# A gated cross-attention and mixture-of-experts block: first batch in halves, last batch's shared gate and up as seven products

## The chip, the cores and the metric

The kernel runs on one core of one Trainium2 chip. The metric is device time in microseconds (us). A core has TensorE (PE; its weight loads are listed apart as PEld), VectorE (DVE), ScalarE (ACT), GpSimd (POOL) and SyncE (SP, which here issues most DMAs). Each engine works through its own instructions in order and waits for the others through semaphores.

## The reference

All data are float32. Four batches of 512 tokens of width 512 go through two sub-blocks, each behind a layer norm and with a residual:

```python
x = x + jnp.tanh(g_xattn[0]) * _L0_xattn_ref(_layernorm(x), fside, ctx)
x = x + jnp.tanh(g_ffn[0]) * _L0_ffn_ref(_layernorm(x), gate_w, w_gate, w_up, w_down, ws_gate, ws_up, ws_down)
```

The first is, for each batch with weights of its own, two linears that are quantised to int8 steps (with a smoothing scale from column maxima and row scales), with silu(gate) * up between them. The second is a mixture of 16 experts over all 2048 tokens together, two experts a token, at most 256 tokens an expert, plus a shared expert that every token passes:

```python
g = jax.nn.silu(jnp.einsum('ech,ehi->eci', buf, w_gate))
u = jnp.einsum('ech,ehi->eci', buf, w_up)
expert_out = jnp.einsum('eci,eih->ech', g * u, w_down)
...
sh = jnp.einsum('ti,ih->th', jax.nn.silu(x @ ws_gate) * (x @ ws_up), ws_down)
```

The shared expert has 704 hidden features: five full chunks of 128 and a rest of 64.

## The kernel before

**Stages.** (1) The opening, batch 0's two linears and its second norm, written out by hand as steps with due times (`opening.at(time, ...)`, sorted and emitted). (2) The middle, batches 1 to 3, whose order a planner fixes while the program is built: each step has an engine, a duration, its needs and a rank, and `Plan` starts from the times at which each engine is taken to come free (`dict(PE=74.5, DVE=76.5, ACT=74.0, POOL=78.0, ...)`). The chain of a batch (first linear, second linear, norm, routing) has low ranks, so it goes first; the shared expert's products of batches 0 to 2 have the highest and fill TensorE between. (3) Sixteen routed experts. (4) The last stage: the shared expert of batch 3, the gathering of the routed results by GpSimd, their addition to X, and the stores.

**Opening, end of the second linear.** For each of four tiles of 128 tokens: `multiplied` (L726, TensorE), `scale` (L732, DVE), `residual` (L739, X + o, on GpSimd unless given DVE), `stats` (L292 and L293, DVE). Then `inv_std` (L270) gives 1/std for all four tiles at once: `begin` on DVE, a square root on ScalarE (L266), `end` on DVE. `normal` (L753, DVE) writes y, `turn_y` transposes it on TensorE (L773) and copies it on ScalarE into xT (L354). Between them `idle` (L1266) emits transposes that nobody reads. Only when all four tiles are in xT does `beside` run the first chunk of the shared expert, four products for gate (pg) and four for up (pu, both L972), each over 512 token columns, with silu (L976) and hT = g * pu (L979). Steps of batch 1's first linear stand among these products: column maxima of x and of its weights (`turn_max`, `wide1.turn`, L299), the smoothing scales s and rs (L316 to L325), their row broadcasts (`row_rs`, `row_s`, L307), then `divide` (L494, DVE) and `multiply` (L499, GpSimd).

**Between middle and experts.** When the last batch is routed, `tokens_of` (L930) sums one-hot products on TensorE into st; DVE turns that into slot_token (L944), GpSimd gathers the tokens of expert 0 (L1105), a DMA transposes them (L391), ScalarE and DVE join them into xgT (L354), and DVE forms sums S of them (L1144 to L1147). A routed expert's gate and up are seven half-size products each over 352 columns (L1154, `gate_up`), with sums on DVE and copies on ScalarE between them: a 2 by 2 block product by seven multiplications.

**Last stage.** Chunk 0 of batch 3's shared expert runs whole. Then 20 buffers are filled by gathers (L1699), the gates of chunks 1 to 4 and the rest (L1011) run, then the four ups, each followed by additions of gathered results (`add_results(upto)`, L1710, counted through 12, 15, 18, 21) and by its hT. The token products (sh, L1037, and L1043 for the rest) follow in two pairs of tiles, with additions up to 28 and 32 and `tokens_add` (L1050) with the stores (L1682). A gather beyond the twentieth is issued when an addition frees a buffer:

```python
def add_results(upto):
    while added[0] < upto:
        j, k = tiles[added[0] // 2], added[0] % 2
        vec.scalar_tensor_tensor(X[:, j, :], yks[added[0]], wk[k][:, j : j + 1], X[:, j, :], ALU.mult, ALU.add)
        if k == 1 and j < NT - TT:
            store(j)
        added[0] += 1
        if len(yks) < 2 * NT:
            gather_result()
```

Of the kernel before, what the change touches and what calls it, by code (L numbers as in the profile page):

```python
# [20 lines left out]
P = 128  # L21
# [99 lines left out]
def flamingo_gated_kernel(  # L121
# [138 lines left out]
    def small(n, name):  # L260
        return stat.tile([P, n], F32, tag=name, name=name)
# [8 lines left out]
    def inv_std(w, h, table=False):  # L270


        def begin():
            w.ve, w.r = small(TT, "ve" + h), small(TT, "r" + h)
            vec.tensor_scalar(w.ve, w.mv[:, :, 1], LN_EPS, None, ALU.add)

        def end():
            if table:
                vec.reciprocal(w.r, w.r)

            c = small(TT, "c" + h)
            vec.tensor_tensor(c, w.r, w.r, ALU.mult)
            vec.scalar_tensor_tensor(c, c, -0.5, w.ve, ALU.mult, ALU.mult)
            vec.scalar_tensor_tensor(w.r, c, 1.5, w.r, ALU.add, ALU.mult)
            w.nmr = small(TT, "nmr" + h)
            vec.scalar_tensor_tensor(w.nmr, w.mv[:, :, 0], -1.0, w.r, ALU.mult, ALU.mult)

        return [begin, lambda: root(w.r, w.ve, neg_half, table), end]
# [151 lines left out]
    def first(b):  # L440
# [27 lines left out]
        def turn_max():  # L468
            v.tp = columns(beside_ps if b == 1 else ps, v.am, HC)
# [146 lines left out]
    def second(b):  # L616
# [190 lines left out]
        v.norm = inv_std(v, "2", table=b == 0)  # L807
        return v
# [154 lines left out]
    def glu_steps(xT, o, dst, home):  # L963


        pl, bufs = home
        v = SimpleNamespace(ps={})

        def product(name, w, k):
            if k == 0:  # L970
                v.ps[name] = ps_mm.tile([P, H], F32, tag="mm", name=name)
            pe.matmul(v.ps[name], lhsT=w[:, k, o : o + P], rhs=xT[:, k, :], start=(k == 0), stop=(k == HC - 1))  # L972

        def silu():
            v.g = pl.tile([P, S], F32, tag="g", name="g", bufs=bufs)
            act.activation(v.g, v.ps["pg"], AF.Silu)  # L976

        def times():
            vec.tensor_tensor(dst, v.g, v.ps["pu"], ALU.mult)  # L979

        gate = [lambda k=k: product("pg", wsg, k) for k in range(HC)]
        up = [lambda k=k: product("pu", wsu, k) for k in range(HC)]
        return gate, silu, up, times
# [7 lines left out]
    def shared(b, done=None):  # L991
        s = SimpleNamespace()

        def chunk_steps(c, home=(shp, 2)):
            if c == 0:
                s.hT = shp.tile([P, len(CHUNKS_IS), S], F32, tag="hT", name="hT")
            return glu_steps(xTs[b], c * P, s.hT[:, c, :], home)
# [254 lines left out]
    f1, (wide1, narrow1) = first(1), weights(1, beside_ps)  # L1252
# [4 lines left out]
    def each(step, *args, ts=range(TT)):  # L1257
        return [lambda t=t: step(t, *args) for t in ts]
# [9 lines left out]
    def idle_x(t):  # L1268
        idle(X[:, t, :])
# [31 lines left out]
    opening.at(53.5, lambda: s0.product(2), lambda: s0.residual(1), lambda: s0.stats(0), lambda: s0.product(3))  # L1301
    opening.at(55.0, lambda: s0.residual(3, vec), lambda: s0.residual(2), lambda: s0.stats(1), lambda: s0.stats(3))
    opening.at(55.1, *each(idle_x, ts=[1, 2, 3]))
    opening.at(58.0, lambda: s0.stats(2), s0.norm[0], *each(lambda t: idle(s0.mv[:, t, 0:1]), ts=[1, 3]), lambda: idle(s0.mv[:, 2, 0:1], 3), s0.norm[1], s0.norm[2], lambda: idle(s0.ve[:, :1], 3))
    for t in range(TT):
        opening.at(61.0 + 0.5 * t, lambda t=t: s0.normal(t, vec), lambda t=t: s0.turn_y(t))
    sh0 = shared(0)

    opening.at(64.0, *each(f1.greater, ts=[1, 2, 3]), *each(wide1.absolute), *each(wide1.greater, ts=[1, 2, 3]))

    def beside():
        gate, silu, up, times = sh0.chunk_steps(0)
        order = gate[:1] + [f1.turn_max] + gate[1:3] + [f1.column_max] + gate[3:] + [wide1.turn, wide1.end]
        order += f1.smooth + [lambda: table(AF.Silu), silu]
        order += up[:2] + [f1.row_rs, f1.row_s, *each(f1.multiply), *each(f1.divide)] + up[2:] + [times]
        for step in order:
            step()


    opening.at(65.0, beside, lambda: s0.keep_normal(TT - 1), lambda: s0.store_normal(TT - 1))  # L1320
    with tc.manual_schedule():
# [5 lines left out]
        dict(PE=74.5, DVE=76.5, ACT=74.0, POOL=78.0, SP=70.0, DMA=70.0, XBAR=70.0),  # L1327
# [257 lines left out]
    plan_shared(0, sh0, [], range(1, FULL), home0)  # L1585
# [101 lines left out]
    with tc.manual_schedule():  # L1687
        chunks = [sh3.chunk_steps(0)]
        for step in chunks[0][0] + [chunks[0][1]] + chunks[0][2] + [chunks[0][3]]:
            step()  # L1690
# [31 lines left out]
        for c in range(1, FULL):  # L1722
            chunks.append(sh3.chunk_steps(c, (results, 4)))
            for step in chunks[c][0] + [chunks[c][1]]:
                step()
# [3 lines left out]
        for c, upto in zip(range(1, FULL), (12, 15, 18, 21)):  # L1729
            for step in chunks[c][2]:  # L1730
                step()
            add_results(upto)
            chunks[c][3]()
            if c == 2:
                sh3.rest_times(0)
                sh3.rest_times(1)

        for u, uptos in enumerate(((28, 28), (2 * NT, 2 * NT))):
# [49 lines left out]
```

## Time and profile before

| what | us |
|---|---|
| runs shown, lowest / median / highest | 576.94 / 586.7 / 592.93 |
| the profiled execution | 580.96 |
| its span | 579.0 |
| busy in the span: PE / DVE / ACT / POOL | 538.2 / 406.4 / 228.0 / 140.8 |
| batch 0's first shared product begins | 63.22 |
| last stage, first product to last addition | 512.13 to 576.12 |

Busy time of TensorE counts each product from its start to a modelled end, so products that follow each other overlap in it: the distance from start to start tells what one costs. A product in float32 appears as two passes, two records. Granted clock is the share of TensorE's full clock. "a <- b" in a list of waits means that a waited for b: us in total, times, longest. A releaser named "issue" or "remote" is one that the profile couldn't name.

### The profile page before, as it was taken

Reading aid. Unit: us, or ns where it says so; the run is one execution under the profiler, and the core shown is the slowest. Engines: PE = TensorE matmul, PEld = TensorE weight load, DVE = VectorE, ACT = ScalarE, POOL = GpSimd, SP = SyncE. Lnnn points to the kernel's source line nnn. Section 1 sums busy time; section 2 is a strip of 40 time slices with the busy share of each in tenths; the row PEclk is TensorE's granted clock in tenths of the full one; section 3 lists DMA queues with packets and bytes.
Section 4 is the critical chain, followed back from the end, with each engine's and each line's share of the span. In section 5 each row is a group of like instructions: output and inputs, shape, how many; then the busy total and the mean of one; then the engine's idle time right before and its main releaser. Section 6 shows DMA issues by size and latency. Waiting matters only on the chain.

```text
span 579.0 us, 5971 instructions
## 1 busy us (share of the span) xinstructions
PE 538.2 (93%) x1830; PEld 283.9 (49%) x1830; DVE 406.4 (70%) x927; ACT 228.0 (39%) x379; POOL 140.8 (24%) x155
## 2 busy tenths in 40 slices
PE   0667799999999999999989999999999999999977
PEld 0544444544444444544455555555555555644422
DVE  6889788999998997985478666665755665315445
ACT  4554577538516353140146254444443444211000
POOL 1315032253261511201321022111111100027740
PEclk9978999999999999999999999999999999999989
DMA  8971012013205092010787999999999995336864
GB/s 283 366 243 37 1 73 72 1 44 82 57 1 109 15 326 68 2 72 3 169 253 219 219 284 282 250 269 271 291 241 261 287 259 144 86 101 199 247 216 164
DMA packets 93967, 95.07 MB, mean 164 GB/s; under 512 B 51552, under 2 KB 70240, under 8 KB 93936
## 3 DMA queue, kind: packets, MB, share of 16 engines
q1 hardware_dynamic: 84064, 69.39, 45.1%
q0 software_dynamic: 5120, 16.78, 9.2%
q10 hardware_dynamic: 4752, 8.52, 3.9%
q8 instruction: 15, 0.25, 0.2%
q14 instruction: 16, 0.13, 0.1%
HBM read 66.36 MB, written 16.78 MB: 144 GB/s over the span
## 4 chain that ended last, share of the span: by engine, by line
PE 75%; DVE 12%; issue 5%; POOL 3%; ACT 1%; DMA 1%; another core or an unknown queue 1%; SPq 0%; DVEq 0%; POOLq 0%
PE b L1154 22%; PE eo L987 14%; PE pg L972 9%; PE sh L1037 9%; PE pu L972 8%; POOL yk L1699 2%; PE pr L1011 2%; PE tp_h L1174 2%; PE acc L576 2%; DVE X L1710 1%; PE rowb L307 1%; PE sh L1043 1%; DVE scx L331 1%; PE acc L726 1%
## 5 line engine op out<-in xcount | busy, mean ns | idle before, releaser
L987 PE MATMUL eo<-wd,ehT 128*128 128x512 f32 (+1 forms) x192 | 85.1, 592 | 0.0
L1105 POOL DMA_INDIRECT xg<-xn_dram,slot_token x32 | 35.7, 1117 | 195.4 <-DMA xp<-xg 160.6
L1037 PE MATMUL sh<-wsd,hT 128*128 128x512 f32 x160 | 75.3, 607 | 4.0 <-DVE hT L979 4.0
L972 PE MATMUL pg<-xT,wsg 128*128 128x512 f32 x160 | 74.9, 597 | 0.7 <-ACT xT L354 0.7
L972 PE MATMUL pu<-xT,wsu 128*128 128x512 f32 x160 | 74.0, 595 | 0.0
L987 PEld LDWEIGHTS eo<-wd,ehT 128*128 128x128 f32 (+1 forms) x192 | 36.4, 190 | 41.6 <-issue 37.0
L354 ACT COPY xgT<-xp 128x1024 int16<-128x1024 int16 x31 | 39.5, 1339 | 27.6 <-DMA xp<-xg 27.6
L1203 DVE TENSOR_TENSOR p<-p,b 128x352 f32<-128x352 f32 x16 | 8.3, 520 | 57.6 <-PE b L1154 57.6
L1037 PEld LDWEIGHTS sh<-wsd,hT 128*128 128x128 f32 x160 | 29.5, 194 | 36.2 <-issue 30.5
L1699 POOL DMA_INDIRECT yk<-eo_dram,slot x32 | 32.6, 1020 | 51.5 <-PE pg L972 42.1
L972 PEld LDWEIGHTS pu<-xT,wsu 128*128 128x128 f32 x160 | 29.2, 190 | 30.8 <-issue 30.6
L972 PEld LDWEIGHTS pg<-xT,wsg 128*128 128x128 f32 x160 | 28.7, 190 | 31.0 <-issue 29.5
L1154 PE MATMUL b<-T,S 128*128 128x352 f32 x128 | 40.6, 460 | 0.7 <-DVE S L1145 0.7
L1154 PE MATMUL b<-wg,xgT 128*128 128x352 f32 x128 | 40.6, 460 | 0.0
L1154 PE MATMUL b<-wu,S 128*128 128x352 f32 x128 | 40.5, 459 | 0.0
L1165 ACT COPY eo_sb<-eo 128x512 f32<-128x512 f32 x32 | 18.7, 585 | 47.4 <-PE eo L987 39.4
L979 DVE TENSOR_TENSOR hT<-g,pu 128x512 f32<-128x512 f32 x20 | 13.6, 682 | 32.1 <-PE pu L972 15.6
L1154 PEld LDWEIGHTS b<-T,S 128*128 128x128 f32 x128 | 24.2, 190 | 14.5 <-issue 1.2
L1154 PEld LDWEIGHTS b<-wu,S 128*128 128x128 f32 x128 | 24.3, 190 | 13.5
L499 POOL TENSOR_TENSOR wi<-wi,s_row 128x512 f32<-128x512 f32 x16 | 19.9, 1272 | 42.5 <-ACT s_row L484 42.5
L1154 PEld LDWEIGHTS b<-wg,xgT 128*128 128x128 f32 x128 | 23.1, 190 | 10.9 <-issue 0.8
L1710 DVE SCALAR_TENSOR_TENSOR X<-yk,wk,X 128x512 f32<-128x512 f32 x32 | 23.4, 751 | 7.0 <-DMA yk<-eo_dram,slot 6.5
(235 smaller groups left out, 866.0 us busy)
## 6 DMA issues: line engine op xcount, KB each, us to landing
wg<-in_L_ffn_w_gate_dram SPq DMA_DIRECT2D x16, 704.0 KB, 7.7
wu<-in_L_ffn_w_up_dram SPq DMA_DIRECT2D x16, 704.0 KB, 6.3
wd<-in_L_ffn_w_down_dram SPq DMA_DIRECT2D x16, 512.0 KB
eo_dram<-eo_sb ACTq DMA_DIRECT2D x32, 256.0 KB, 2.0
X<-in_x_dram SPq DMA_DIRECT2D x16, 256.0 KB, 6.5
xn_dram<-yp SPq DMA_DIRECT2D x16, 256.0 KB, 2.0
out_dram<-X SPq DMA_DIRECT2D x15, 256.0 KB, 2.0
wi<-in_fside_BxS2xS_dram SPq DMA_DIRECT2D x3, 1024.0 KB
```

What stands on the lines that cost most here:

```text
L354: return (vec.tensor_copy if on is vec else act.copy)(dst, src)
L499: on.tensor_tensor(w.wi[:, t, :], w.wi[:, t, :], v.s_row, ALU.mult)
L576: pe.matmul(accs[t], lhsT=block(b, w.xqT, k, t), rhs=block(b, w.wqT, k), start=(k == 0), stop=(k == HC - 1))
L972: pe.matmul(v.ps[name], lhsT=w[:, k, o : o + P], rhs=xT[:, k, :], start=(k == 0), stop=(k == HC - 1))
L979: vec.tensor_tensor(dst, v.g, v.ps["pu"], ALU.mult)
L987: pe.matmul(acc, lhsT=hT[:m, c, bass.ts(t, P)], rhs=wd[:m, c, :], start=(c == 0), stop=(c == len(chunks) - 1))
L1037: pe.matmul(accs[t], lhsT=s.hT[:, c, bass.ts(t, P)], rhs=wsd[:, c, :], start=(c == 0), stop=(c == last))
L1105: pool.indirect_dma_start(out=xg.rearrange("p l n -> p (l n)"), out_offset=None, in_=xn_dram, in_offset=bass.IndirectOffsetOnAxis(ap=slot_ ...
L1154: pe.matmul(ps[:, :I], lhsT=lhs[:, k, :], rhs=rhs[:, k, :], start=(first and k == 0), stop=(k == HALF - 1), skip_group_check=not first,)
L1165: act.copy(eo, R[e].acc[h])
L1699: pool.indirect_dma_start(out=yk, out_offset=None, in_=eo_dram, in_offset=bass.IndirectOffsetOnAxis(ap=slot[i % 2][:, tiles[i // 2] : tile ...
L1710: vec.scalar_tensor_tensor(X[:, j, :], yks[added[0]], wk[k][:, j : j + 1], X[:, j, :], ALU.mult, ALU.add)
```

## The change

Opening: from the second linear's end on, the tiles go in two halves. `inv_std` takes a slice of tiles; residual(1) moves from GpSimd to DVE; tiles 0 and 1 are normalised and transposed before tiles 2 and 3 have their statistics; most idle transposes there are gone. `beside` runs two chunks of the shared expert, each product split into 256 columns for the first two tiles and 256 for the last two: three half groups, the turns of tiles 2 and 3, and then the other five with batch 1's steps among them. The planner starts from later times and has one chunk fewer of batch 0. Batch 1's column maxima take one of the two banks of another pool.

Last stage: for each of the five chunks, gate and up (two products of 512 features by 128 for 512 tokens) become one 2 by 2 block product by seven multiplications: fourteen products of 256 columns, with four differences of weights and six sums or products of results on DVE and three copies and two silu on ScalarE. `combine_tokens` (four DVE operations of 128x512) and the first `combine_weights` come before. The additions of results are counted through 3, 5, 8, 11, then 24 and 32.

```diff
-    opening.at(53.5, lambda: s0.product(2), lambda: s0.residual(1), lambda: s0.stats(0), lambda: s0.product(3))
-    opening.at(55.0, lambda: s0.residual(3, vec), lambda: s0.residual(2), lambda: s0.stats(1), lambda: s0.stats(3))
-    opening.at(55.1, *each(idle_x, ts=[1, 2, 3]))
...
+    opening.at(52.5, lambda: s0.residual(1, vec), lambda: idle_x(1), lambda: s0.stats(1), lambda: s0.stats(0), lambda: idle_x(0))
+    early, late = s0.norms
+    opening.at(55.0, early[0], early[1], lambda: s0.product(2), lambda: idle(s0.mv[:, 0, 0:1]), lambda: s0.residual(2), lambda: s0.multiplied(3), early[2])
+    for t in (0, 1):
+        opening.at(56.0, lambda t=t: s0.normal(t, vec), lambda t=t: s0.turn_y(t))
+    opening.at(57.0, lambda: s0.scale(3), lambda: s0.residual(3, vec), lambda: s0.stats(2), lambda: s0.stats(3), *late)
...
+        (gate0, silu0, up0, times0), (gate1, silu1, up1, times1) = (sh0.chunk_steps(c, in_halves=True) for c in range(2))
+        turns = [step for t in (2, 3) for step in (lambda t=t: s0.normal(t, vec), lambda t=t: s0.turn_y(t))]
+        order = gate0[0] + up0[0] + gate1[0] + turns + up1[0]
+        order += [*each(f1.greater, ts=[1, 2, 3]), f1.turn_max, *each(wide1.absolute), *each(wide1.greater, ts=[1, 2, 3])]
+        order += gate0[1] + [f1.column_max] + up0[1] + [wide1.turn, wide1.end] + gate1[1] + f1.smooth
+        order += [lambda: table(AF.Silu), silu0, silu1] + up1[1][:2] + [f1.row_rs, f1.row_s, *each(f1.multiply), *each(f1.divide)]
+        order += up1[1][2:] + [times0, times1]
...
-        dict(PE=74.5, DVE=76.5, ACT=74.0, POOL=78.0, SP=70.0, DMA=70.0, XBAR=70.0),
+        dict(PE=76.5, DVE=78.0, ACT=75.5, POOL=79.0, SP=70.0, DMA=70.0, XBAR=70.0),
...
-    plan_shared(0, sh0, [], range(1, FULL), home0)
+    plan_shared(0, sh0, [], range(2, FULL), home0)
...
+            def chunk(c, upto):
...
+                product(b1, Bg, A11, True)
+                act.copy(p1, b1)
+                product(b2, Dg, A12, True)
+                vec.tensor_tensor(p1, p1, b2, ALU.add)
+                act.activation(g1, p1, AF.Silu)
+                product(b1, T2, S2, False)
+                act.copy(u2, b1)
+                if c + 1 < FULL:
+                    combine_weights(c + 1, range(2))
+                product(b3, T1, S1, True)
+                vec.tensor_tensor(u2, u2, b3, ALU.add)
+                product(b1, T3, S3, False)
+                act.copy(u3, b1)
+                if c + 1 < FULL:
+                    combine_weights(c + 1, range(2, 4))
+                product(b4, Du, S4, True)
+                vec.tensor_tensor(u3, u3, b3, ALU.add)
+                vec.tensor_tensor(u2, u2, b4, ALU.add)
+                vec.tensor_tensor(hT[:, :N], g1, u2, ALU.mult)
+                product(b1, T4, A22, False)
+                act.activation(g2, b1, AF.Silu)
+                add_results(upto)
+                vec.tensor_tensor(hT[:, N:], g2, u3, ALU.mult)
...
+        halves.chunk(0, 0)
         for k in range(HC):
             sh3.rest_product(k)
         sh3.rest_silu()
...
+        for c, upto in zip(range(1, FULL), (3, 5, 8, 11)):
+            halves.chunk(c, upto)
+
+        for u, uptos in enumerate(((24, 24), (2 * NT, 2 * NT))):
```

## The prediction

> **What bounds the kernel now.** I read the table of stretches first, because one share over the whole span mixes stages; columns: busy us and count of TensorE (PE), weight loads (PEld), DVE, ACT, POOL, then granted clock, DMA share, GB/s.
>
> ```profile
> 48.00:58.00 10.00, 6.96 (x39) 4.04 (x40) 9.23 (x22) 4.63 (x6) 4.79 (x4) 0.91 0.16 53
> 58.00:63.00 5.00, 4.08 (x25) 3.03 (x23) 4.49 (x14) 2.19 (x5) 0.00 (x0) 0.83 0.00 0
> 63.00:75.00 12.00, 9.84 (x40) 4.64 (x40) 9.02 (x22) 8.18 (x16) 1.76 (x2) 1.00 0.01 3
> 250.00:270.00 20.00, 20.00 (x69) 9.20 (x68) 14.62 (x55) 3.62 (x6) 0.00 (x0) 1.00 0.07 26
> 550.00:560.00 10.00, 7.98 (x21) 3.04 (x19) 2.77 (x4) 0.00 (x0) 6.24 (x7) 1.00 0.86 282
> 560.00:570.00 10.00, 8.05 (x16) 3.64 (x17) 8.65 (x13) 0.00 (x0) 0.00 (x0) 0.83 0.44 162
> ```
>
> From 63 us on TensorE is full; only the opening (DVE at 9 of 10 us, TensorE doing "idle" transposes) and the stretch after 550 are not. The list of TensorE's waits names what is left:
>
> ```profile
> PE rowb L307 <- DVE rs L325: 6.5, 3, 2.7
> PE sh L1037 <- DVE hT L979: 4.0, 1, 4.0
> PE tp_q L361 <- ACT xq L351: 1.8, 4, 1.1
> ```
>
> So work taken from TensorE counts one for one, if nothing else ends a stage. The timeline shows where something else does, at the first expert:
>
> ```profile
> 271.47 0.35 PE L930 MATMUL st<-colt,rows 128*128 128x32 f16 x8
> 272.92 1.20 POOL L1105 DMA_INDIRECT xg<-xn_dram,slot_token  x1 [30.37 <-DVE slot_token L944]
> 280.85 1.33 ACT L354 COPY xgT<-xp 128x1024 int16<-128x1024 int16 x1 [16.76 <-DMA xp<-xg]
> 282.55 1.13 PE L1043 MATMUL sh<-wsd,hT 64*128 64x512 f32 x4
> 283.61 2.63 PE L1154 MATMUL b<-wg,xgT 128*128 128x352 f32 x8
> 286.34 0.43 DVE L1145 TENSOR_TENSOR S<-S,xgT 128x256 f32<-128x256 f32 x1
> 286.91 0.53 PE L1154 MATMUL b<-T,S 128*128 128x352 f32 x1 [0.67 <-DVE S L1145]
> ```
>
> The routing's last product (st) releases gather, transpose and copy: the first xgT is complete at 282.18, 10.7 us after st. TensorE covers these us with shared products of batch 2 that end at 283.6, just in time. Last, the end:
>
> ```profile
> 550.69 0.69 DVE L979 TENSOR_TENSOR hT<-g,pu 128x512 f32<-128x512 f32 x1 [3.55 <-issue]
> 561.21 0.69 DVE L979 TENSOR_TENSOR hT<-g,pu 128x512 f32<-128x512 f32 x1 [7.71 <-remote]
> ```
>
> DVE stood still for 3.55 and 7.71 us before two products whose inputs were ready (the last pu began at 549.5). The profile doesn't name the releaser; gathers and stores fill the DMA engines meanwhile. Of the 11.3 us, 4.0 reached TensorE.
>
> **Part 1, opening.** Up to the second linear's scale(0) at 50.58 nothing moves. After it DVE runs scale(1) to 52.0, then residual(1), now on DVE beside POOL's residual(0). The row for that combination:
>
> ```profile
> 51.41 3.74 POOL L739 TENSOR_TENSOR X<-X,o 128x512 f32<-128x512 f32 x3 [1.54 <-DVE o L732]
> 54.30 1.40 DVE L739 TENSOR_TENSOR X<-X,o 128x512 f32<-128x512 f32 x1
> ```
>
> DVE's residual took 1.40 us and ended when POOL's third (begun about 53.9) had been over for half a us. [...] Sum on DVE: two stats of 0.85 to 55.0, ve 0.2, scale(2) 0.72, four small ones of 0.2 to 56.75, block to 57.25, two normals of 0.48 to 58.2. Then transposes (0.6) and ACT's copy (0.55): first shared product at 59.6 (58.9 without the lock), where before it began at 63.22: 3.6 us earlier.
>
> A 512-column product is two passes of 0.43 us (in the chain, 8 passes take 3.44), 0.857 in all; 352 columns take 0.293 a pass, so 0.83 ns a column, 0.213 a pass for 256, if weight loads keep up. The nearest row is the 64-column product L872/L873, whose loads follow each other after 0.11 us (176.89, 177.00): under 0.213. Halving costs nothing; the other end, 0.24 a pass, is 0.9 us over 32 more passes.
>
> From 59.6: three half groups 5.1, transposes of tiles 2 and 3 0.9, group 1.7, turn_max 0.45, two groups 3.4, wide1.turn 0.45: 71.6. From that turn to rs DVE and ACT took 3.8 us before (67.6 to 71.4): rs at 75.4, 4.0 later than before. TensorE has 2.6 us of work meanwhile and waits 1.3, where it waited 1.95. The rest (row broadcasts 1.1, half a group) ends at 77.3 where before it was 74.2. That is 3.1 us later with one chunk (6.86) more done: TensorE is 3.7 us ahead, but batch 1's chain, which goes on from rs, is 4.0 us behind. Queued behind rs: POOL's four multiplies (4.97 us), DVE's divides, ACT's xq, and TensorE's tp_q, which already waited 1.8 us for xq; I add 1 us there (ends 0 and 2.7).
>
> **What the lead buys.** The order of TensorE's instructions is fixed when the program is built, and I counted it in both programs. Between st and the first expert product stand 11 shared products and two rest pairs before (11 x 0.857 + 2 x 1.07 = 11.6 us), 2 and one in the changed one (2.8 us). So 8.8 us of filler now stand ahead of st, and 0.9 us of transposes have moved behind the first shared product. st comes at 271.5 - 3.6 (earlier start) + 8.8 + 0.9 - 0.65 (shorter wait) + 1 (tp_q) = 278. After st 10.7 us pass until xgT, filler covers st's 0.2 and 2.8, so TensorE stands 7.7 us; then two products (2.3) at full clock, and the S product at st + 13.1 instead of + 15.4: 291.1 against 286.9. The hole has a second price: in 560:570 the granted clock was 0.83 after a wait of 4.0 us. [...] I take 1.7: experts start 5.9 us later. Bounds: -1.5 (no stall anywhere after 59.6) to +8.
>
> **Part 2, end.** Forty 512-column products (34.3 us) become seventy of 256 (70 x 0.427 = 29.9): 4.4 us less. DVE gets per chunk four differences of weights and six of results at 0.42 (the 128x256 rows L1144 to L1147) for one product of 0.69, besides 2 or 3 result additions of 0.735: 5.7 to 6.4 us a chunk, against 5.98 on TensorE. The additions stand before the second half of hT, and behind them in DVE's queue is the next chunk's p1 sum, for which ACT's Silu and then its copy of b1 wait, and TensorE's third product on b1. With 3 additions that sum runs at 2.7 to 3.1 us of a chunk; Silu 0.42 and copy 0.38 end at 4.0, TensorE wanted b1 at 3.4. About 0.7 to 1 us for two or three chunks: 2.3. Then 21 additions are left (11 before), 15.4 us, with tokens_add 2.9 us, against 19.2 us of TensorE: DVE ends last, 57.0 us after the first product. Undisturbed, the old order gives 34.3 + 3.4 + 17.1 + 2.1 + 1.1 = 58.0; it took 64.0 (512.13 to 576.12). combine_tokens (4 x 0.69) lies beside the last experts' products, where DVE has 30 to 50% free; combine_weights(0) beside 7.7 us of down products; without that cover both would cost 4.4. Gathers stay 20 ahead (POOL 1.25 to 1.39 each). So -1.0, or -7.0 if DVE's unexplained stop does not return. Nothing in the edit removes it; I keep it.
>
> **Sum.** The profiled execution took 580.96 (span 579.0 and 2 around it): 581 + 5.9 - 1.0 = 586, a ratio of 1.009. The runs shown (576.94 to 592.93) have their median 1% above it: 586.7 x 1.009 = 592; I say 591.
>
> **Cases.**
> - Likeliest, 0.47: as summed, 0 to 1.6% slower, 586 to 596.
> - Rival, slower, 0.24: DVE's stop in the gather stage. DVE is now the tight engine there, so its 11.3 us reach TensorE whole instead of 4.0 (with half clock 6): 586 - 6 + 11.3 = 591 to 593, on the median's footing 597 to 600. It decides once DVE stops longer than the slack of a chunk, about 0.5 us. For it: DVE's busy sum; against: the stops came late, beside stores.
> - Rival, faster, 0.2: the stop doesn't return and batch 1's chain catches up: 581 - 7 + 0 to - 1.5: 573, 578 on the median's footing. For it: only one place of the plan has to give; against: st's place in the order.
> - The change doesn't do what it says, 0.09: the first half is held (ports, clock at half from 56 to 60) until 62 or so; no lead and the same 9.7 us in front of st: 590 to 603.
>
> About 2% (12 us) is what a measurement of this kernel can tell from no change, its runs being 16 us apart. Faster by that needs the third case and luck: 0.13. Slower: most of the second, half of the fourth, and the upper end of the first: 0.33. Within: 0.54. Range 577 to 603, from the third case to the end of the fourth.
>
> **What would show it.** First pg near 59.6 and logit near 77; st near 278 with a TensorE wait of 6 to 8 us for ACT's xgT and a clock below 1 there; 14 products of 0.427 a chunk at the end, with waits of 0.5 to 1 us on ACT's copy. I am wrong if experts start before 286, if 256-column passes are 0.24 apart, or if the end stage is under 56 us.

## The result and the profile after

| what | before | after |
|---|---|---|
| median of 6 runs, us | 577.14 | 605.85 |
| lowest to highest | 575.91 to 592.93 | 605.11 to 606.72 |
| ratio, 95% interval | | 1.0508 [1.0491, 1.0525] |
| profiled execution's span | 579.0 | 604.1 |
| first product of the experts begins | 283.61 | 293.83 |
| last stage's first product begins | 512.13 | 524.34 |
| DVE's last addition ends | 576.11 | 601.25 |

The changed kernel is 5% slower where the prediction said 591 us. By the last three rows the 25 us between the two spans lie in three places: 10.2 before the experts, 2.0 within them, 12.9 in the last stage (64.0 us before, 76.9 after). A repetition, told below, measured 583.5 us with a last stage of 55.2 us: the loss there comes on some occasions of measurement and not on others, and this result was taken on one with it.

The stretches of the changed kernel, in the columns shown before (busy us and count of TensorE, weight loads, DVE, ACT, POOL, then granted clock, DMA share, GB/s):

```profile
48.00:58.00 10.00, 6.65 (x33) 3.85 (x32) 8.60 (x21) 4.84 (x7) 3.52 (x3) 0.83 0.17 53
58.00:63.00 5.00, 3.19 (x13) 2.56 (x14) 4.49 (x13) 1.28 (x3) 0.06 (x1) 0.77 0.00 0
63.00:75.00 12.00, 12.00 (x63) 10.50 (x62) 6.39 (x14) 3.26 (x7) 0.00 (x0) 0.95 0.00 1
...
285.00:295.00 10.00, 2.45 (x7) 1.14 (x7) 3.02 (x6) 1.33 (x1) 4.33 (x7) 0.72 0.60 136
295.00:305.00 10.00, 10.00 (x27) 5.93 (x25) 4.80 (x9) 3.46 (x6) 2.31 (x3) 0.77 0.98 227
540.00:550.00 10.00, 4.69 (x12) 3.52 (x12) 1.26 (x4) 0.37 (x1) 7.56 (x9) 0.66 0.72 209
550.00:560.00 10.00, 0.00 (x0) 0.00 (x0) 3.35 (x6) 0.38 (x1) 5.58 (x6) 0.61 0.57 164
```

TensorE is now full from 63 us (12.00 of 12), as the change means it to be. But it stands in two new places, 285 to 295 us (2.45 of 10) and 540 to 560 us (4.69 of 20), and its granted clock is down at both. Its timeline shows the three stops:

```profile
283.05 0.36 PE L936 MATMUL st<-colt,rows 128*128 128x32 f16 x8
283.25 1.96 PE L1051 MATMUL sh<-wsd,hT 128*128 128x512 f32 x4
285.15 1.13 PE L1057 MATMUL sh<-wsd,hT 64*128 64x512 f32 x4
293.83 5.03 PE L1168 MATMUL b<-wg,xgT 128*128 128x352 f32 x8 [7.55 <-issue]
...
538.22 1.03 PE L1743 MATMUL b<-xgT,wsu 128*128 128x256 f32 x4
545.05 2.07 PE L1743 MATMUL b<-xT,T 128*128 128x256 f32 x4 [5.81 <-issue]
546.92 2.82 PE L1743 MATMUL b<-xT,wsg 128*128 128x256 f32 x8
561.36 1.22 PE L1743 MATMUL b<-xgT,T 128*128 128x256 f32 x2 [11.62 <-ACT p L1757]
```

The first is the hole behind the routing that the prediction names: 7.55 us, followed by eight passes that take 5.03 us where they took 2.63. The other two lie in the second and third of the five chunks. ACT and DVE show what they wait for:

```profile
544.62 0.37 ACT L1768 COPY u<-b 128x256 f32<-128x256 f32 x1 [7.43 <-remote]
558.71 0.38 ACT L1776 ACTIVATE g<-b 128x256 f32<-128x256 f32 x1 [13.72 <-remote]
560.94 0.37 ACT L1757 COPY p<-b 128x256 f32<-128x256 f32 x1 [1.84 <-remote]
```

```profile
545.03 0.42 DVE L1772 TENSOR_TENSOR u<-u,b 128x256 f32<-128x256 f32 x1 [4.19 <-issue]
553.08 0.42 DVE L1773 TENSOR_TENSOR u<-u,b 128x256 f32<-128x256 f32 x1 [7.63 <-issue]
```

DVE's sum at L1773 needs the product of the row at 538.22, which ended at 539.25. It began at 553.08, with DVE idle for 7.63 us and nothing named as releaser. In the trace that instruction waits for TensorE's semaphore; the trace holds no record of the update that let it go (between 544.60 and 558.69 it has none of this semaphore). TensorE had nothing else to do from 539.25 to 545.05. ACT's silu at L1776 waits in the same way for a product that ended at 547.12 and is signalled at 558.69. So it is TensorE's signal of a finished product that comes late, by 11.6 and 13.8 us, while GpSimd issues gathers (one every 1.25 us from 528.19 to 552.00, then three more to 557.79). The ends of products are modelled, so a product that itself ended late would look alike; but TensorE went on at 546.92 with the eight passes behind its product of 545.05 without a pause.

DVE's two stops in the profile of before (3.55 and 7.71 us) look the same. The last three ups are one row there:

```profile
539.59 10.46 PE L972 MATMUL pu<-xT,wsu 128*128 128x512 f32 x24
```

The third chunk's up ended at 546.62 and the fourth's at 550.05; their hT began at 550.69 and 561.21, 4.1 and 11.2 us later. The updates of TensorE's semaphore stand at 561.18 and 561.38, the one before these at 529.47, though seven products had ended in between. TensorE itself ran on until 557.98 on other products.

### The profile page after: what moved, and what is told of

The parts are those of the page before. It is cut to its first block, busy times and chain, and to the rows that moved or that the text cites. A ratio compares the mean times of both kernels' runs of the same rounds, so it can differ in the third digit from the quotient of the medians.

```text
span 604.1 us, 6215 instructions
## 1 busy us (share of the span) xinstructions
PE 539.7 (89%) x1904; PEld 304.8 (50%) x1908; DVE 427.2 (71%) x981; ACT 233.9 (39%) x400; POOL 138.6 (23%) x154
## 4 chain that ended last, share of the span: by engine, by line
PE 72%; DVE 13%; issue 5%; another core or an unknown queue 4%; ACT 2%; POOL 2%; DMA 1%; SPq 0%; DVEq 0%; POOLq 0%; ACTq 0%
PE b L1168 22%; PE eo L1001 14%; PE sh L1051 9%; PE pu L978 6%; PE pg L978 6%; PE b L1743 4%; PE pr L1025 2%; PE tp_h L1188 2%; PE acc L581 1%; DVE scx L336 1%; DVE xn L499 1%; PE sh L1057 1%; PE rowb L312 1%; PE tp_q L366 1%
## 5 line engine op out<-in xcount | busy, mean ns | idle before, releaser
L1119 POOL DMA_INDIRECT xg<-xn_dram,slot_token x32 | 34.3, 1073 | 197.4 <-DMA xp<-xg 162.6
L1051 PE MATMUL sh<-wsd,hT 128*128 128x512 f32 x160 | 73.7, 597 | 0.0
L978 PE MATMUL pg<-xT,wsg 128*128 128x512 f32 (+1 forms) x136 | 58.3, 560 | 1.5 <-ACT xT L359 1.5
L978 PE MATMUL pu<-xT,wsu 128*128 128x512 f32 (+1 forms) x136 | 56.5, 544 | 0.0
L1168 PE MATMUL b<-wg,xgT 128*128 128x352 f32 x128 | 43.0, 481 | 7.5 <-issue 7.5
L978 PEld LDWEIGHTS pg<-xT,wsg 128*128 128x128 f32 x136 | 25.7, 198 | 21.8 <-issue 17.9
L978 PEld LDWEIGHTS pu<-xT,wsu 128*128 128x128 f32 x136 | 24.8, 190 | 19.9 <-issue 19.1
L1743 PE MATMUL b<-xgT,T 128*128 128x256 f32 x60 | 16.4, 428 | 11.8 <-ACT p L1757 11.6
L744 POOL TENSOR_TENSOR X<-X,o 128x512 f32<-128x512 f32 x12 | 15.5, 1310 | 43.4 <-DVE o L737 39.5
```

The costliest lines, as they stand in the source:

```text
L744: on.tensor_tensor(Xb[:, t, :], Xb[:, t, :], os_[t], ALU.add)
L978: pe.matmul(v.ps[name][:, ts], lhsT=w[:, k, o : o + P], rhs=xT[:, k, ts], start=(k == 0), stop=(k == HC - 1))
L1051: pe.matmul(accs[t], lhsT=s.hT[:, c, bass.ts(t, P)], rhs=wsd[:, c, :], start=(c == 0), stop=(c == last))
L1119: pool.indirect_dma_start(out=xg.rearrange("p l n -> p (l n)"), out_offset=None, in_=xn_dram, in_offset=bass.IndirectOffsetOnAxis(ap=slot_ ...
L1168: pe.matmul(ps[:, :I], lhsT=lhs[:, k, :], rhs=rhs[:, k, :], start=(first and k == 0), stop=(k == HALF - 1), skip_group_check=not first,)
L1743: pe.matmul(ps, lhsT=w[:, k, :], rhs=x[:, k, :], start=(first and k == 0), stop=(k == HALF - 1), skip_group_check=not first,)
```

## The experiments

Kernels measured on one occasion ran on one chip, beside the kernel before. Occasions differed: on three (this result's, and two below) the kernel before scattered up to 592 or 595 us and late signals stand in the traces; on five others it stayed within 574.2 to 578.6 and no trace shows such a stop. One chip had them on one occasion and not on a later one, so the chip alone doesn't decide. "With late signals" below means this. A second mark agrees. In the seven traces of those three occasions, 14 to 34 updates of DVE's and ACT's semaphores have no record within 0.05 us of the instruction's end, most of them while the gathers run; in the thirteen traces of the other five every one has. Each run listed has a span and a clock of its own profile, so whether the recording itself has a part in the late signals was not separated.

### The two parts, one at a time

Edit of e1: the changed opening and middle, the last stage of before. Edit of e2: the reverse. Both on one occasion, without late signals.

> The changed opening (halves from the second linear's end, shared products of two chunks among the turns, the planner's new start times) with the last stage of before. The kernel before is 577.1. Theory: the two parts of the loss are independent, and the opening alone brings the 12.2 us by which the changed profile reaches the last stage later: 587 to 591. Rival: the two parts hang together (a slower clock carried from one to the other), or the opening costs only the 5.9 us of the prediction: 581 to 585.

> The opening of before with the changed last stage (seven products a chunk, gathered rows added later). Theory: TensorE's signals of finished products reach DVE and ACT up to 12 us late while GpSimd issues gathers one after the other at 1.25 us each, and in the new order each chunk needs such a signal before it can go on; so this part alone brings the other 12 to 13 us, waits of TensorE of about 6 and 12 us among the first three chunks and its half clock behind them: 588 to 592. Rival: the prediction's sum for this stage, -1.0 us: 575 to 578, the waits having come from the changed opening.

e1: 587.6 us, ratio 1.0189 [1.0172, 1.0206], 11.0 us slower. e2: 573.1 us, 0.9939 [0.9921, 0.9957], 3.4 us faster. The theory held for the opening and fell for the last stage: the new order alone had no stop at all, gathers 1.25 us apart or not. From first product to last addition it took 55.2 us, the old order 58.5 (e1). Then the whole kernel should give 584.

### The changed kernel again, with and without a space between gathers

Edit of e6 (and, on the kernels of e3, e4, e12 and e14, the same):

```diff
+        pause = results.tile([P, 256], F32, tag="pause", name="pause", bufs=1)
...
             )
+            pool.memset(pause, 0.0)
             yks.append(yk)
```

> The changed kernel itself, once more, beside the kernel before (576.5 in the runs so far). Its two parts alone gave +11.0 us (opening) and -3.4 us (last stage), 584 together. Theory A (what made the last stage 17 us longer in the changed kernel's own runs, TensorE's late signals, belongs to those runs or their chip, since the kernel before showed it there too, and neither part alone has it here): 583 to 586, no wait of TensorE over 3 us after the last stage's first product. Theory B (the two parts together bring the late signals about, by where the gathers fall against the products): 604 to 607 again, with waits near 6 and 12 us.

> The changed kernel with a filled tile of 128x256 after each gather of result rows, so that gathers start about 1.45 us apart in place of 1.25 (as measured with this spacing). If theory A holds: 2 to 3 us above the run before it, as the spacing cost with the old opening (575.8 against 573.1), so 586 to 589. If theory B holds and GpSimd's unbroken stream is what holds the signals back: the waits go and it gives 586 to 589 where the run before it gives 605; if B holds and the spacing has no part in it, 605 to 608.

e5: 583.5 us, 1.0141 [1.0097, 1.0185], the sum of the two parts; last stage 55.2 us, no stop. e6: 587.2 us. So theory A: the 22 us that the result has more are not a property of the two parts together.

> As the run before it, with one thing added: after each gather of result rows GpSimd fills a tile of 128x256 that nobody reads (about 0.3 us by GpSimd's rows of 0.10 us for one column and 0.20 us for 128), so that gathers start some 1.55 us apart in place of 1.25. Same data, same products, same additions. Theory (GpSimd's unbroken stream holds TensorE's signals back, while at the 1.39 to 1.45 us apart of the first third of the stream in the kernel before they came on time): the waits of 6 and 12 us go, the last stage takes 57 to 61 us in place of 77, and the kernel 570 to 576. Rival: the new order's own handshakes or the weight of the additions on DVE make the waits, and the spacing changes nothing: 588 to 592, or more since gathers end later.

> The kernel before with that filled tile after each gather and nothing else. Theory: DVE's two stops of 3.55 and 7.71 us ahead of hT are the same late signals; they go, TensorE loses neither the 4 us nor the half clock behind them, and the last stage takes 58 to 60 us in place of 64: 571 to 574. Rival: the stops come from elsewhere, and the later gathers only push the additions back: 577 to 581.

> The changed kernel with the filled tile of 128x256 after each gather of result rows (spacing 1.45 us), once more. The late signals of TensorE came on two occasions, both times with the kernel before scattered up to 592 us beside it, and on two others not at all, with the kernel before within 574.9 to 578.6. If this is an occasion without them: 586 to 588 as measured. If it is one with them (the kernel before scattered above 580), theory: they need GpSimd's unbroken stream at 1.25 us, so here no stop of TensorE over 3 us in the last stage, 586 to 592; rival: the spacing has no part in it, stops of 5 and 12 us again, 603 to 609.

These three fell on occasions without late signals and could only show what the space costs there. e3: 575.8, 2.7 us above e2, since the last gathers come later and the additions behind them (last stage 58.5 us). e4: 576.0 beside 576.5 for the kernel before, 0.9992 [0.9982, 1.0002]: the space costs the old order nothing. e12: 586.5 as e6.

Then one occasion had late signals, the kernel before at 574.7 to 594.7 on it, and the comparison could be made:

> The opening of before with the changed last stage, once more (573.1 before, where no late signals came). On an occasion without late signals: 572 to 574 again. On one with them (the kernel before scattered above 580 us beside it): stops of about 5 and 12 us in the second and third chunk as in the changed kernel there, 590 to 596.

> The same with the filled tile of 128x256 after each gather of result rows (575.8 before). On an occasion without late signals: 575 to 577 again. On one with them: theory (they need the unbroken stream at 1.25 us), no stop over 3 us, 575 to 580; rival (the spacing has no part in it), 592 to 598.

e13, the new last stage without the space: 594.0 us (592.8 to 594.3). e14, with it: 576.2 us in 20 runs, 574.2 to 577.8, on the same occasion. The stretches of e13 and of e14 from the last stage's first product on:

```profile
513.00:523.00 10.00, 10.00 (x40) 7.23 (x39) 3.97 (x10) 2.86 (x7) 4.76 (x5) 1.00 0.42 120
523.00:533.00 10.00, 6.29 (x27) 5.09 (x26) 3.54 (x9) 1.69 (x5) 7.57 (x8) 0.96 0.72 209
533.00:543.00 10.00, 2.97 (x8) 2.02 (x6) 2.92 (x5) 0.00 (x0) 7.67 (x8) 0.67 0.72 209
543.00:553.00 10.00, 3.20 (x8) 2.62 (x9) 1.61 (x4) 1.54 (x4) 1.89 (x2) 0.52 0.32 92
```

```profile
512.00:522.00 10.00, 10.00 (x40) 7.22 (x39) 4.08 (x11) 2.80 (x7) 5.90 (x9) 1.00 0.39 111
522.00:532.00 10.00, 9.86 (x46) 8.36 (x45) 8.82 (x21) 2.88 (x8) 8.84 (x15) 1.00 0.61 179
532.00:542.00 10.00, 10.00 (x49) 8.78 (x48) 8.61 (x19) 2.97 (x8) 9.01 (x13) 1.00 0.60 172
542.00:552.00 10.00, 9.85 (x32) 5.79 (x31) 7.91 (x15) 1.43 (x4) 8.84 (x15) 1.00 0.66 187
```

Read column POOL: 8 gathers in 10 us and nothing else in e13, 7 gathers and as many fills in e14. In e13, with gathers 1.25 us apart, TensorE falls to 2.97 of 10 us and a granted clock of 0.67, then 0.52; in e14, with 1.44 us from gather to gather, it is busy 9.85 to 10.00 of 10 us at 1.00. DMA traffic differs by a seventh (209 against 179 GB/s). The profiled execution of e14 has the second mark too (34 updates of DVE and ACT without a record), so it ran under the same condition. With the fill after each gather the stops were gone in this pair of runs. Whether that is by the time between gathers, by the slower flow of bytes, or because GpSimd does something else in between, these two runs don't tell apart. In the five traces with long stops (the result, e9, e10, e13, e15) TensorE's first began 11.0 to 11.1 us after the first gather, about when the ninth ended; since gathers and products have nearly the same phase in all five, that may be the place of the product as well as the number of the gather.

> The opening of before and the changed last stage, with each gather taking half as many bytes: 128 rows of 256 numbers in place of 512, of a table seen as twice as many half rows. So the sums at the end are not the reference's; each addition is made in two halves from the one half row. As many gathers, descriptors and waits as before. If the late signals come from the bytes that land: gone on an occasion with them too, 572 to 576. If they come from GpSimd's issuing one gather after the other: on such an occasion (the kernel before scattered above 580 us beside it) stops as long as in the run of 594.0, 588 to 595. On an occasion without them it tells nothing: 571 to 575.

```diff
-                out=yk,
+                out=yk[:, : H // 2],
...
-                in_=eo_dram,
+                in_=eo_dram.rearrange("r (two c) -> (r two) c", two=2),
```

e17, which leaves out half of each gathered row, fell on an occasion without late signals, so bytes and issues were not told apart. It took 577.8 us, its additions being made in two halves. What joins GpSimd's gathers to TensorE's signals stays open.

### Where the loss before the experts comes from

> The changed opening with only the first chunk's gate and up among the turns (in halves); the second chunk goes back to the planner's filler, as in the kernel before, at the changed start times; last stage of before. Beside it stands the changed opening alone, 587.6, where the routing's last product stands at 284.3 us against 271.6 before, and the second batch's logits 8 us later than before. Theory (the second chunk's 32 passes of 0.21 us stand in TensorE's order ahead of the column maxima and row scales on which the second batch's chain waits): that chain starts 3 to 6 us earlier, the whole is 581 to 585. Rival (what is lacking is the filler that the second chunk would have been ahead of the experts): the idle time of 7.4 us before the first expert's products is filled, but with the routing as late as before the whole stays at 586 to 589.

```diff
-        order = gate0[0] + up0[0] + gate1[0] + turns + up1[0]
+        order = gate0[0] + turns + up0[0]
...
-    plan_shared(0, sh0, [], range(2, FULL), home0)
+    plan_shared(0, sh0, [], range(1, FULL), home0)
```

e7: 592.9 us, 5.3 above e1. Both the theory and the rival fell: with the second chunk gone from the opening, DVE's copy of the second batch's logits came later still (155.7 us against 154.1 in e1), and the experts at 300.2 (e1: 294.8).

> The changed opening with the third residual on DVE in place of GpSimd, last stage of before; beside the changed opening alone, 587.6. In the changed kernel GpSimd's third residual (56.80 to 58.06 us) ran beside DVE's 128x2 operation of the inverse root, which took 1.25 us in place of 0.16, ahead of the first normal. Theory (that wait moves the whole chain): DVE takes 0.72 us for the residual, the small operation 0.16, the first shared product comes 0.5 to 1.1 us earlier, the whole 586 to 587. Rival: DVE is the engine that the opening waits for, its own 0.72 us push the normals back as far as the wait did: 587.5 to 589.

```diff
-lambda: s0.residual(2), lambda: s0.multiplied(3)
+lambda: s0.residual(2, vec), lambda: s0.multiplied(3)
```

e8: 585.2 us (584.1 to 587.5) where e1 gave 587.6 on another occasion. In e8's timeline of DVE the small operation is back at 0.16 us:

```profile
56.66 0.69 DVE L744 TENSOR_TENSOR X<-X,o 128x512 f32<-128x512 f32 x1
57.46 0.16 DVE L286 TENSOR_TENSOR c<-r 128x2 f32<-128x2 f32 x1
```

and the first shared product came 9.09 us after the second linear's first `scale`. In the six other executions of the same opening (the changed kernel, e1, e5, e6, e11, e12) it came 9.88 to 10.63 us after it. So the 1.25 us of the small operation went with GpSimd's residual beside it, and this part of the opening gets shorter by about 0.8 us or more; that the whole kernel gains from it is not shown, since the occasions differ.

> The changed kernel (583.5 in its second measurement) with one reordering in the opening: ACT's absolute values of the second batch's weights, and DVE's maxima of them, are issued before the second half's turns instead of behind them, the turn of the maxima and the row scales follow earlier in TensorE's order, and silu and the up products of the second chunk come later. Nothing is added or taken away. In the changed kernel ACT stood 6.69 us at the copies of the second half's turns (67.86 us), which TensorE does behind three groups of half products; the absolute values, on tiles long there, began at 68.82 us against 63.06 before, DVE then idled 4.96 us, and TensorE's row scales came at 78.07 against 71.46. Theory (that place in ACT's queue is what sets the second batch's chain back, and with it the routing before the experts): absolute values from about 61 us, row scales at 71.5 to 73.5 us, the routing's last product 6 to 10 us earlier than 282, the kernel 573 to 578. Rival 1 (the chain was late already by the late turns of the second half, or falls back to the planner's order anyway): row scales move, the routing does not, 581 to 584. Rival 2 (the turns, now behind the absolute values, starve the second halves' products): 583 to 587.

```diff
-        order = gate0[0] + up0[0] + gate1[0] + turns + up1[0]
-        order += [*each(f1.greater, ts=[1, 2, 3]), f1.turn_max, *each(wide1.absolute), *each(wide1.greater, ts=[1, 2, 3])]
+        order = gate0[0] + up0[0] + [lambda t=t: s0.normal(t, vec) for t in (2, 3)]
+        order += [*each(wide1.absolute), *each(f1.greater, ts=[1, 2, 3]), *each(wide1.greater, ts=[1, 2, 3])]
+        order += gate1[0] + [lambda t=t: s0.turn_y(t) for t in (2, 3)] + [f1.turn_max] + up1[0][:4] + [f1.column_max]
...
```

> The run before it with the third residual on DVE in place of GpSimd as well (which alone gave 585.2 against 587.6 with the old last stage, on another chip). Theory: it takes the 1.1 us that the 128x2 operation stood beside GpSimd from the way to the first shared product: 1 to 2 us below the run before it. Rival: DVE, now without its idle stretch of 4.96 us, is what the opening waits for, and the 0.72 us come back: equal or up to 1 us above.

Both ran with late signals (604.2 and 604.1 us), so they are read by their traces before 300 us. The row scales moved, 78.62 to 76.02 us, and the routing did not: DVE's copy of the second batch's logits at 152.5 and 152.8 us (152.5 in the changed kernel), the experts at 293.3 and 294.2 against 293.8. Rival 1 held. e10's third residual on DVE changed nothing there either (experts later by 1 us).

> The changed kernel with one number of the planner changed: the slack that it allows TensorE after a dependency in the second batch, 0.9 us in place of 0.6. Its order then leaves 14 of the shared products behind the routing's last product and ahead of the first expert's, where the changed kernel leaves 4 (counted as instructions of 512 columns with both passes, and without the rest pairs; the kernel before leaves 15). Theory (the loss outside the last stage lies in how many shared products the planner's order puts ahead of the routing, since TensorE works through them without a stop of over 1.6 us from 86 us to the routing's last product): that product stands at 271 to 276 us in place of 282 to 284, the stop of 7.5 us before the first expert product falls to 1 us or less, the half clock of 6.8 us behind it goes, and the whole is 6 to 10 us below the changed kernel on the same chip: 574 to 578 where that is 583.5. Rival (the second batch's chain itself is late, so that TensorE waits for it wherever it stands in the order): new stops of together 6 us or more between 100 and 275 us, and no gain over 2 us.

```diff
-        plan.margin = {1: 0.6, 2: 1.5, 3: 0.9}[b]
+        plan.margin = {1: 0.9, 2: 1.5, 3: 0.9}[b]
```

e11: 586.4 us, against 583.5 for the changed kernel on another occasion. Its timeline of TensorE behind the routing's last product:

```profile
285.61 0.35 PE L936 MATMUL st<-colt,rows 128*128 128x32 f16 x8
285.89 1.13 PE L1057 MATMUL sh<-wsd,hT 64*128 64x512 f32 x4
286.95 8.85 PE L1051 MATMUL sh<-wsd,hT 128*128 128x512 f32 x20
295.73 1.13 PE L1057 MATMUL sh<-wsd,hT 64*128 64x512 f32 x4
296.79 2.63 PE L1168 MATMUL b<-wg,xgT 128*128 128x352 f32 x8
```

The hole is gone, filled to the last microsecond, and the clock behind it is whole (eight passes in 2.63 us). But st stands at 285.6, later than before the edit, and e11's list of TensorE's waits from 85 to 300 us shows where the time went instead:

```profile
PE tp_x L778 <- ACT y L760: 5.1, 3, 3.8
PE rowb L312 <- DVE scw L343: 4.0, 1, 4.0
```

The longest wait for ACT's y, 3.8 us, ends at 141.0. DVE is what is full there, in part because two small operations of the chain take 1.2 us each beside GpSimd, in place of 0.16:

```profile
135.00:145.00 10.00, 5.03 (x19) 2.34 (x17) 9.76 (x17) 4.82 (x7) 4.70 (x4) 0.86 0.07 26
```

```profile
136.11 3.71 POOL L504 TENSOR_TENSOR wi<-wi,s_row 128x512 f32<-128x512 f32 x3
137.43 1.18 DVE L287 SCALAR_TENSOR_TENSOR c<-c,ve 128x4 f32<-128x4 f32 x1
138.65 1.19 DVE L288 SCALAR_TENSOR_TENSOR r<-c,r 128x4 f32<-128x4 f32 x1
```

The wait of 4.0 us, which ends at 237.5, is of another kind: DVE itself stood there, for GpSimd.

```profile
235.92 1.22 DVE L703 TENSOR_REDUCE scw<-wc 128x4 f32<-128x1024 f32 x1 [5.60 <-POOL wc L653]
```

The theory fell, and the rival's figures held: 9 us of new stops and no gain. TensorE waits for its chains wherever they stand in the order, and the filler only decides whether the idle time lies at 140 and 235 us or at 286. Only the first of these stops lies in the second batch's chain.

> The changed kernel with both edits that alone did nothing: the absolute values and maxima of the second batch's weights ahead of the second half's turns (row scales 2.4 us earlier, routing not), and the planner's slack of 0.9 us for the second batch (14 shared products left behind the routing, but new stops of 4.0 and 3.8 us in that batch). Theory (the second batch's chain is late from the opening on, and the order decides only where TensorE then idles): with the chain 2 to 3 us earlier the new stops shrink by as much, 2 to 3 us below the 586.4 of the second edit alone on an occasion without late signals: 583 to 584.5. Rival (the planner's order alone sets it, and by chance moves either way): no change, 586 to 587, the stops as long as before. Late signals would add about 20 us; then the stops before 300 us are to be compared.

e15 had late signals (606.9 us). Before 300 us it has stops of 3.6 and 4.6 us in place of 4.0 and 5.1, and the experts at 296.1 in place of 296.8: 0.7 us, not 2 to 3. So the two edits together don't bring the chain back.

### The new last stage with a space after the middle gathers

> The opening of before, the changed last stage, and the filled tile only after the gathers from the seventh to the twenty-second, so that the stream ends some 4 us earlier than with one after each (576.2 with, 573.1 without where there are no late signals, 594.0 without where there are). Theory (the late signals begin 10.6 us after the first gather, when the ninth is issued, and the additions space the last ones out by themselves): 573 to 575 on any occasion, no stop over 3 us. Rival (gathers that start 1.25 us apart anywhere in the stream bring them on): 573 to 575 without late signals, 580 or more with them.

> The run of 574.7 again, with the space after the seventh to twenty-second gather only. On an occasion without late signals: 573 to 576. On one with them (the kernel before scattered above 580 us): theory, 574 to 577 and no stop over 3 us; rival (the unspaced gathers at both ends bring them on), 580 or more.

```diff
             )
+            if 6 <= i < 22:
+                pool.memset(pause, 0.0)
             yks.append(yk)
```

The opening of before, the new last stage and this: 574.7 us, 0.9969 [0.9947, 0.9990], and 573.8 us, 0.9968 [0.9955, 0.9980], 0.3% faster than before. Neither occasion had late signals. Without any space the stage gives 573.1 us there and 594.0 with them; with a space after every gather 575.8 and 576.2, which is 0.9991 [0.9977, 1.0005] and 0.9970 [0.9942, 0.9997] of the kernel before. Whether a space after the middle gathers alone is enough with late signals was not seen.

## Why the prediction was wrong

The sum had the experts 5.9 us later and the last stage 1.0 us shorter. The result has 12.2 (10.2 before the experts and 2.0 within them) and 12.9 us longer.

**Last stage.** The sum for an undisturbed stage was right in kind: a 256-column pass every 0.216 us (0.213 said) and DVE's additions reaching the end. It gave 58.0 us for the old order and 57.0 for the new; e1 and e2 show 58.5 and 55.2, so the gain is 3.3 us and not 1.0, and the stage is under the 56 us that the prediction named as a sign of being wrong. The old order was sized well; the term that was too large is the new order's. Its waits on ACT's copies were put at 2.3 us, and e2 lists none of TensorE in the stage: the five chunks took 31.0 us where 29.9 and 2.3 were said. And the parts that it lists (29.9, 3.4 for the rest, 2.3, 15.4 and 2.9) make 53.9 us, not 57.0.

The step that failed is the one that kept DVE's unexplained stop as a constant ("nothing in the edit removes it; I keep it") and gave its growth, as the slower rival, 0.24 and 597 to 600 us. That rival is nearest to what the result shows, and its mechanism was half seen: the stop did reach TensorE whole. But the prediction took it for a fixed 11.3 us of DVE. By the trace it is a delay of TensorE's own signals, and in the result three consumers met it: ACT's copy (begun at 544.62 after 7.43 us of idle time), DVE's sum (553.08) and ACT's silu (558.71). The old order asks for few in that stretch, four ups in a row whose results only DVE's hT needs; the new one has in each chunk a way from TensorE to ACT and back, and one from TensorE to DVE. So two stops of 5.8 and 11.6 us came on TensorE, with a granted clock of 0.50 from 542.0 to 548.7 us and from 552.3 to 565.8: 64.0 us became 76.9. A size could not be taken from the one trace of before. That the cause could be absent, the faster case (0.2) had allowed; the runs shown, 576.94 to 592.93, were taken for scatter and used to raise the number by 1%. Without late signals the whole kernel's ratio (e5: 1.0141) lies in the likeliest case's 0 to 1.6%, but by luck: the opening costs 11.0 us and not 5.9, and the last stage gains 3.4 and not 1.0.

**Opening.** That DVE loses time beside GpSimd was put on the right engines and at the wrong operation. The prediction let GpSimd's third residual block the first normal, to 57.25 us (0.7 us of the first shared product's 59.6); no run shows that term, which the fourth case carries on to 62 us. In the result the first two normals took 0.50 us each, after that residual had ended, and the operation that stands beside it is the 128x2 one ahead of them:

```profile
56.80 1.26 POOL L744 TENSOR_TENSOR X<-X,o 128x512 f32<-128x512 f32 x1 [3.95 <-DVE r L283]
56.82 1.25 DVE L286 TENSOR_TENSOR c<-r 128x2 f32<-128x2 f32 x1
58.51 1.00 DVE L758 TENSOR_SCALAR y<-X,mv,r 128x512 f32<-128x512 f32 x2
```

1.25 us in place of 0.16 (its later twin at 63.18). The residual that moved to DVE took 1.21 us beside GpSimd's (51.58 to 52.85) and ended at 53.40, where the sum's two stats to 55.0 need it at 53.3; DVE's next one, at 60.20 with GpSimd idle, took 0.69. Ahead of the third scale DVE had stood 0.63 us for the third tile's product (L731), which the sum had without a wait. The first shared product came at 60.93 us, not 59.6. Then:

```profile
60.93 3.55 PE L978 MATMUL pg<-xT,wsg 128*128 128x256 f32 x8 [0.71 <-ACT xT L359]
64.31 1.89 PE L978 MATMUL pu<-xT,wsu 128*128 128x256 f32 x8
...
78.62 0.62 PE L312 MATMUL rowb<-ident,rs 128*128 128x128 f32 x4 [1.16 <-DVE rs L330]
...
80.47 1.07 PE L791 MATMUL logit<-xT,gateT 128*32 128x512 f32 x8
```

The first half group took 3.4 us and not 1.7, at a granted clock of 0.50 from 60.8 to 64.1 us (0.77 over 58 to 63), which the prediction priced only behind the routing. With these 1.3 and 1.7 us the row broadcast stands at 78.6 (said: 75.4) and the logits at 80.5 (said: 77.3). TensorE's lead from the second chunk (6.86 us) is then 0.6 us, not 3.7.

**Before the experts.** The hole itself was sized well: 7.7 us said, 7.55 found, and the clock behind it, 1.7 us said, is near the 2.0 us by which the experts took longer. The 1.7 was the author's estimate from one row of before, 0.83 over 560 to 570 us (0.17 of 10 us); in the result the granted clock was 0.50 from 289.5 to 299.6 us, and eight passes took 2.40 us more than before (5.03 and 2.63). What failed is the place of st, 278 said, 283.05 found: 3.1 us are the opening's, and most of the rest are small waits in the middle, for which the prediction allowed 1 us at tp_q. The waits listed for TensorE from 79 to 283 us sum to 1.4 us before and 3.8 after. Added up, the first expert product is later by 7.55 (hole) - 0.6 (lead) + 2.4 (waits) = 9.4 of the 10.2 us; 0.8 us remain unassigned. The step that failed as a whole is "what the lead buys": the sum treated the order of TensorE's instructions as the thing that sets st. In e11 a different order only moved the place where TensorE idles. Why the chain, 6.4 us late at DVE's copy of batch 1's logits, is 11.4 us late at that of the last batch's, was not settled; e7, e9, e11 and e15 speak against the second chunk, the place of the maxima in ACT's queue and the place of the filler, each as the sole cause.

## What to carry to other kernels

A stop that the profile leaves unexplained need not be a constant: here it was 11.3 us of DVE in one trace, 17.4 us of TensorE in another (5.81 and 11.62 in the result) and none of TensorE in a third (e2). Ask which signal is late, and count how many such signals the new order needs at once in that stretch. Work pulled forward from the filler is worth only what a chain leaves uncovered; if the chain gets later by what TensorE gains, the idle time comes back where the filler is missing. Where the runs of one kernel lie 16 us apart, measure the parts and the whole again on another occasion before explaining a difference.

## What the runs showed of the hardware

- In the result DVE's sum that waits for TensorE's semaphore began 13.8 us after the modelled end of its product (539.25 to 553.08), while GpSimd issued indirect gathers of 128 rows of 2 KB every 1.25 us. Behind ACT's copy there was no such delay (it ended at 545.00, TensorE began at 545.05). With a fill after each gather and 1.44 us from gather to gather, on an occasion that brought it otherwise, it was not seen (e14), and on five of eight occasions not at all. Why an occasion has it is open.
- Three small operations of DVE that stood beside one of GpSimd took 1.25 us (128x2, the changed kernel) and 1.18 and 1.19 us (128x4, e11). Without it the first took 0.16 us (e8, and its twin at 63.18 in the changed kernel), and the lines of the other two took 0.16 each, also on 128x4, at 50.27 and 50.46 us of the changed kernel, with GpSimd idle.
- TensorE's granted clock in the result was 0.50 from 289.5 to 299.6 us, around the end of the stop of 7.55 us at 293.83. It was 0.77 over 295 to 305 us, where TensorE was busy all 10 us, and eight passes took 5.03 us in place of 2.63.
